# Four graph layers in one kernel: edges on 128 partitions, a bank for layer 1's weights, one record a step at layer 0's end, later outputs in layer 3

## The chip, the cores and the metric

The kernel runs on one core of a Trainium2 chip, in one launch. The time is the device time of that launch in microseconds (us). The kernel before took 3802.98 us as the median of ten runs (3795.99 to 3816.99).

A core has TensorE (PE, matrix products; its weight loads are shown apart as PEld), VectorE (DVE), ScalarE (ACT), GpSimd (POOL) and SyncE (SP). SP and ACT start plain DMAs here. POOL starts the indirect ones: a gather reads one row of a table in device memory for each of up to 128 partitions, by an index that each partition holds, and a scatter writes such rows. [...] Sixteen DMA engines move the data.

## What is computed

A graph of N = 3125 nodes with 256 features and E = 53125 edges, sorted by `dst`, goes through four layers. Each layer reads `h` and its output is added to `x`:

```python
edge_index = jnp.stack([src, dst])
h = jnp.maximum(_layernorm(x, axis=-1), 0.0)
x = x + L0(h, edge_index, edge_attr_64, ...)
h = jnp.maximum(_layernorm(x, axis=-1), 0.0)
x = x + L1(h, edge_index, edge_type_64, ...)
h = jnp.maximum(_layernorm(x, axis=-1), 0.0)
x = x + L2(h, edge_attr_64, ..., edge_index)
h = jnp.maximum(_layernorm(x, axis=-1), 0.0)
x = x + L3(h, edge_index, ...)
```

Cut to what matters here:

```python
# L0: a message for each edge, summed at its dst, then a network for each node
m = relu(concat([h[src], h[dst], edge_attr]) @ eW1 + eb1) @ eW2 + eb2
agg = segment_sum(m, dst)
out = layer_norm(h + mlp(concat([h, agg])), gamma, beta)
# L1: attention with 4 heads and 64 relations, softmax over the edges of a dst
mod_k = K[src] + 0.2 * rel_w[edge_type][:, None, :]
w = softmax over each dst of (Q[dst] * mod_k).sum(-1) / 8
out = layer_norm(segment_sum(w * V[src], dst) @ Wo + bo + h) * gamma + beta
# L2: attention with 8 heads; sums go to the SOURCE side, softmax over all edges
dst, src = edge_index[0], edge_index[1]
key = k[src] + edge_attr @ We + be
out = segment_sum(v[src] * softmax((q[dst] * key).sum(-1) / sqrt(32), axis=0), dst) + bias
# L3: graph attention with one head, then an LSTM step from a zero state
agg = segment_sum(softmax over each dst of leaky_relu(a_src[src] + a_dst[dst]) * xp[src], dst)
i, f, g, o = split(tanh(agg + bias) @ W_ih.T)
out = sigmoid(o) * tanh(sigmoid(i) * tanh(g))
```

## The kernel before

**Two orders of the edges.** Layers 0, 1 and 3 sum at `dst`. The nodes are sorted by degree into 25 blocks of 128, and a node's edges become its slots: for slot s of block b one gather brings one row for each of the block's 128 nodes. Layer 2 sums at the source, so it needs the edges grouped by blocks of 128 sources. For that every edge gets a record of 66 numbers (64 attributes, the address of its dst's row, its source's number in the block), and all records are written into a table `ss` in device memory, source block by source block (`TILES` tiles of 128 records each).

**`prelude`.** The edges lie on `EP` = 125 partitions in `EC` = 425 columns (125 × 425 = 53125). `dst_i`, `e_src`, `e_typ` and `nxt_i` (dst of the next edge, to check the sorting) are loaded so. `counted` (L325 to L334) counts degrees: DVE compares the columns with 128 low and 25 high values (`ol`, `oh`), and PE multiplies the two one-hot sets, a product for each column, in two halves. From the degrees come the rank of every node, the table `a_d` of layer 0's source-side products, the slots (`st`) and `row2`, the place of every edge's record in `ss`. `sfill` fills the whole of `ss` with empty records before, in 40 DMAs from SP. At the end `flag` tells whether the input fits the planned sizes; a branch on it chooses `by_slots` (it does here) or `by_blocks`.

**`by_slots`, the records.** `loaded(c)` loads the attributes of `CH` = 5 columns into a rec buffer by a DMA from SP (L588), `filled` writes the other two fields on DVE (L592, L593), and `scatter_src(n)` (its call of `scatter` is recorded at L158) writes n columns: one indirect scatter for each column, 125 records of 264 bytes, 425 in all. There are two rec buffers; a chunk is loaded at column 1 and filled at column 3 of the one before it. `Kit.queued` keeps POOL's indirect DMAs in the order in which the program writes them, so the places named below are places on POOL's queue.

**Layer 0** runs 226 steps, each for two slots: two gathers `gt` (L154), from the 19th step on one `scatter_src(1)`, four products `ph` on PE (L924), the addition of `gt` to `ph` and the sum into `acc` on DVE (L938, L943), and a `clock.tick()`, by which the node work of earlier blocks goes on in small pieces (`front`, `turned`, `back`). `hp` and `xh` are the node rows that this work loads by SP. When the steps are through, `while clock.busy()` finishes the last block's node work, with `scatter_src(2)` at each tick.

**Layer 1** goes through the slots in 115 shares of up to four gathers `kv` (`scored`), and spreads what is left of the scatters evenly over the shares, less eight that come after the last. `weighed` forms the softmax weights `wt` and the weighted sum: DVE multiplies the weights into kv (L1030), PE adds the slots into `acc` (L1034). `acc` and `wt` are two parts of one PSUM bank, `acc1`. `transposed` turns 128 x 256 node rows through a PSUM tile of its own, `pt`; the products after it use `pm`, two banks.

**Layer 2** reads `ss` by source blocks (`srec`), 594 KB a block. **Layer 3** gathers a row `xg` for each of 439 slots; `block` is a generator that a tick after each gather moves on, each `yield n` letting n ticks pass. It ends with the gated result `gg` (L1457, L1458), `yield 3`, and the scatter to the output, which stands on POOL among the next block's gathers.

Of the kernel before, what the change touches and what calls it, by code (L numbers as in the profile page):

```python
# [9 lines left out]
F32 = mybir.dt.float32  # L10
# [40 lines left out]
assert sum(TILES) == NT  # L51
XH = 516
# [9 lines left out]
class Kit:  # L62
# [67 lines left out]
    def transposed(self, pool, psum, x, name, bufs=2):  # L130

        p = psum.tile([P, 4, P], F32, name="pt", bufs=bufs)
        for k in range(2):
            self.nc.tensor.transpose(p[:, k, :], x[:, k * P:(k + 1) * P], self.ident)  # L134
        t = pool.tile([P, 2, P], F32, name=name)
        self.nc.scalar.copy(t, p[:, 0:2, :])
        return t
# [86 lines left out]
class Lists:  # L224


    def __init__(self, pool):
# [9 lines left out]
        self.row2 = pool.tile([EP, EC], I32, name="row2")  # L237
        self.dst_e = pool.tile([EP, EC], F32, name="dst_e")
        self.srcl_e = pool.tile([EP, EC], F32, name="srcl_e")
# [3 lines left out]
def prelude(ctx, tc, a, a_d, nodes_d, ss, st_d, flag, t):  # L243
# [9 lines left out]
    dst_i = c.tile([EP, EC], I32, name="dst_i")  # L253
    nc.sync.dma_start(dst_i, a["dst"].rearrange("(p c) -> p c", c=EC))
# [5 lines left out]
    e_src = c.tile([EP, EC], I32, name="e_src")  # L260
    nc.scalar.dma_start(e_src, a["src"].rearrange("(p c) -> p c", c=EC))
    e_typ = c.tile([EP, EC], I32, name="e_typ")
    nc.scalar.dma_start(e_typ, a["edge_type_64"].rearrange("(p c) -> p c", c=EC))
    nxt_i = c.tile([EP, EC], I32, name="nxt_i")
    nc.gpsimd.memset(nxt_i, N)
    for p0, p1, w in ((0, EP - 1, EC), (EP - 1, EP, EC - 1)):
        nc.scalar.dma_start(nxt_i[p0:p1, 0:w],
                            bass.AP(tensor=a["dst"].tensor, offset=a["dst"].offset + p0 * EC + 1,
                                    ap=[[EC, p1 - p0], [1, w]]))
# [6 lines left out]
    sfill = c.tile([P, 11, SREC], F32, name="sfill")  # L276
# [12 lines left out]
    nc.gpsimd.memset(cap[:, NB - 1:NB], float(P * TILES[NB - 1]))  # L289
    none = c.tile([1, 512], F32, name="none")  # L290
# [13 lines left out]
    for i in range(40):  # L304
        nc.sync.dma_start(ss[i * 11 * P:(i + 1) * 11 * P, :].rearrange("(p r) c -> p (r c)", p=P),
                          sfill.rearrange("p r c -> p (r c)"))

    both_e = c.tile([EP, EC, 2], I32, name="both_e")
    nc.gpsimd.tensor_copy(both_e[:, :, 0], e_src)
    nc.gpsimd.tensor_copy(both_e[:, :, 1], e_typ)  # L310
    nc.scalar.dma_start(st_d.rearrange("(p c) -> p c", c=2 * EC), both_e.rearrange("p c i -> p (c i)"))


    lo_i = wk.tile([EP, EC], I32, name="lo_i", tag="edge", bufs=4)
    nc.vector.tensor_scalar(lo_i, dst_i, 127, None, op0=ALU.bitwise_and)
    lo = c.tile([EP, EC], BF, name="lo")
    nc.vector.tensor_copy(lo, lo_i)
    hi_i = wk.tile([EP, EC], I32, name="hi_i", tag="edge", bufs=4)
    nc.vector.tensor_scalar(hi_i, dst_i, 7, None, op0=ALU.logical_shift_right)
    hi = c.tile([EP, EC], BF, name="hi")  # L320
    nc.vector.tensor_copy(hi, hi_i)
    pdeg = ps.tile([P, NB], F32, name="pdeg")
    CW = 214

    def counted(hp, c0, c1):  # L325
        w = c1 - c0
        ol = hp.tile([EP, P, CW], BF, name="ol")
        oh = hp.tile([EP, NB, CW], BF, name="oh")
# [4 lines left out]
        for i in range(w):  # L333
            nc.tensor.matmul(pdeg, ol[:, :, i], oh[:, :, i], start=(c0 + i == 0), stop=(c0 + i == EC - 1))  # L334
# [33 lines left out]
    with tc.tile_pool(name="ph", bufs=1) as hp:  # L368
# [3 lines left out]
        counted(hp, CW, EC)  # L372
# [73 lines left out]
    sl_i = wk.tile([EP, EC], I32, name="sl_i", tag="edge", bufs=4)  # L446
    nc.vector.tensor_scalar(sl_i, e_src, 127, None, op0=ALU.bitwise_and)
    nc.vector.tensor_copy(t.srcl_e, sl_i)
    hs_i = wk.tile([EP, EC], I32, name="hs_i", tag="edge", bufs=4)
    nc.vector.tensor_scalar(hs_i, e_src, 7, None, op0=ALU.logical_shift_right)  # L450
    hs = c.tile([EP, EC], BF, name="hs")
    nc.vector.tensor_copy(hs, hs_i)
    eq = op.tile([EP, NB, EC], BF, name="eq")
# [3 lines left out]
    zero = ps.tile([EP, EC], F32, name="zero")  # L457
    nc.vector.memset(zero, 0.0)
    cum = op.tile([EP, NB, EC], F32, name="cum")
# [8 lines left out]
    tots = c.tile([EP, NB], F32, name="tots")  # L468
    nc.vector.tensor_copy(tots, cum[:, :, EC - 1])
    pc3 = ps.tile([P, 4, NB], F32, name="pc3")  # L470
    pc2, pv = pc3[:, 0:2, :], pc3[0:1, 2, :]
    nc.tensor.matmul(pc2[:EP, 0, :], k.tri[:EP, :EP], tots, start=True, stop=True)
    nc.tensor.matmul(pc2[:, 1, :], k.ones[:EP, :], tots, start=True, stop=True)
    viol = wk.tile([EP, EC], F32, name="viol", tag="edge", bufs=4)
    nc.vector.tensor_tensor(viol, dst_i, nxt_i, ALU.is_gt)
    v1 = c.tile([EP, 1], F32, name="v1")
# [5 lines left out]
    nc.vector.tensor_tensor(over, pc2[:, 1, :], cap, ALU.is_gt)  # L482
    v3 = c.tile([P, 1], F32, name="v3")
    nc.vector.tensor_reduce(v3, over, AX.X, ALU.add)
    nc.tensor.matmul(pv[:, 0:1], v1, k.ones[:EP, 0:1], start=True, stop=False)
# [5 lines left out]
    bases = c.tile([EP, NB], F32, name="bases")  # L491
    nc.vector.tensor_scalar(bases, pc2[:EP, 0, :], -1.0, None, op0=ALU.add)
# [4 lines left out]
    for b in range(NB - 1, -1, -1):  # L497
        k.gather(t.st[:, b, 0:SLOTS[b], :].rearrange("p s i -> p (s i)"), flat(st_d, 2 * E), t.off_i[:, b:b + 1], axis=1)
# [46 lines left out]
    pos_i = wk.tile([EP, EC], I32, name="pos_i", tag="edge", bufs=4)  # L545
    nc.vector.tensor_copy(pos_i, cum[:, 0])
    pa_i = wk.tile([EP, EC], I32, name="pa_i", tag="edge", bufs=4)
    nc.vector.tensor_scalar(pa_i, pos_i, 127, None, op0=ALU.bitwise_and)
    pj_i = wk.tile([EP, EC], I32, name="pj_i", tag="edge", bufs=4)
    nc.vector.tensor_scalar(pj_i, pos_i, 7, None, op0=ALU.logical_shift_right)  # L550
    step = wk.tile([EP, EC], F32, name="step", tag="edge", bufs=4)
# [3 lines left out]
    nc.vector.scalar_tensor_tensor(t.row2, hs, float(P * TM), step, op0=ALU.mult, op1=ALU.add)  # L555
    nc.vector.tensor_scalar(t.dst_e, dst_i, float(KVQ), None, op0=ALU.mult)
# [3 lines left out]
def by_slots(ctx, tc, a, out, a_d, nodes_d, ss, t):  # L560
# [19 lines left out]
    attr = a["edge_attr_64"].rearrange("(p c) k -> p c k", c=EC)  # L580
# [16 lines left out]
    def scatter_src(n):  # L597

        for _ in range(n):
            c = done[0]  # L600
            if c == EC:
                return
# [1785 lines left out]
```

## Time and profile before

| what | us |
|---|---|
| median of ten runs | 3802.98 |
| profiled execution | 3803.74 |
| its span | 3801.9 |
| prelude | 0 to 241 |
| layer 0, start and steps | 241 to 1252 |
| layer 0, end | 1252 to 1416 |
| layer 1 | 1416 to 2335 |
| layer 2 | 2335 to 3029 |
| layer 3, node rows | 3030 to 3086 |
| layer 3, edges | 3086 to 3801.9 |

The granted clock of TensorE was 0.779 of full speed on the mean. Over the whole span PE was busy 2401.0 us, DVE 2389.3, ACT 1093.0 and POOL 2481.9, so no engine looks like the bound by its share of 63 to 65%; the stages have different ones. Issuing an indirect DMA costs POOL some 0.30 us more that the profile counts as idle ("issue") and not as busy. A wait line such as "DVE kv L1030 <- PE acc L1034" says that DVE, before an instruction that writes kv at line 1030, stood idle until PE's instruction on acc at line 1034 was done; the numbers after it are the total, how often, and the longest. A DMA issue of `rec` is one plain DMA; its packets are the pieces that the engines move.

### The profile page before, as it was taken

The numbers are of one execution on the slowest core, as the hardware profiler recorded it, in microseconds if no ns is written. First come the engines' busy times: TensorE is split into PE (matmuls) and PEld (weight loads), VectorE is DVE, ScalarE is ACT, GpSimd is POOL, SyncE is SP. The second block draws the span as 40 slices with busy tenths as digits, with TensorE's granted clock in tenths as the row PEclk, the third lists the DMA queues.
The fourth block names the chain that finished last, engine by engine and source line by source line (L and its number), as shares of the span: only waits on it lengthen the run. The fifth ranks groups of instructions, "written<-read, shape, count | busy, mean of one in ns | idle before, by whom it ended". The sixth has DMA issues, their size and how long they took to land. (4 is left out here: it accounts for less than half of the span.)

```text
span 3801.9 us, 32547 instructions
## 1 busy us (share of the span) xinstructions
PE 2401.0 (63%) x9174; PEld 1477.6 (39%) x9174; DVE 2389.3 (63%) x4836; ACT 1093.0 (29%) x2292; POOL 2481.9 (65%) x2497
## 2 busy tenths in 40 slices
PE   5827878788777544677676665898989731112123
PEld 3313434344333223555454443666666520001011
DVE  5646567576666325777777674898988924434444
ACT  1112122222221002222222222676766520112122
POOL 3447677777777775666667553676667446566664
PEclk9858889899998755667877777999999965555556
DMA  6345465665655336666666554666666443333332
GB/s 224 128 128 171 134 182 163 172 181 169 179 168 171 83 93 180 179 189 191 198 184 194 163 160 168 192 202 207 201 207 196 128 128 100 89 99 100 95 103 73
DMA packets 295839, 595.89 MB, mean 157 GB/s; under 512 B 113501, under 2 KB 154508, under 8 KB 295650
## 3 DMA queue, kind: packets, MB, share of 16 engines
q0 software_dynamic: 163616, 472.86, 41.8%
q1 hardware_dynamic: 131512, 119.79, 10.4%
q8 instruction: 76, 1.25, 0.1%
q10 hardware_dynamic: 522, 1.06, 0.1%
q14 instruction: 113, 0.93, 0.1%
HBM read 510.85 MB, written 82.21 MB: 156 GB/s over the span
## 5 line engine op out<-in xcount | busy, mean ns | idle before, releaser
L158 POOL DMA_INDIRECT s_src_records<-rec,row x425 | 512.4, 1206 | 131.6 <-issue 122.5
L154 POOL DMA_INDIRECT kv<-s_l_rows,dst x440 | 456.0, 1036 | 214.5 <-issue 70.4
L924 PE MATMUL ph<-wm,st 128*128 128x512 f32 x904 | 471.0, 648 | 128.5 <-DVE acc L943 61.6
L154 POOL DMA_INDIRECT gt<-s_l_src,srcb x452 | 433.9, 960 | 176.2 <-issue 109.4
L154 POOL DMA_INDIRECT kv<-s_l_kv,st x439 | 419.2, 955 | 177.6 <-issue 107.9
L154 POOL DMA_INDIRECT xg<-s_l_rows,src x439 | 415.7, 947 | 133.7 <-issue 133.7
L1034 PE MATMUL acc<-kv,ident 128*128 128x256 f32 x878 | 305.4, 506 | 118.7 <-DVE kv L1030 118.5
L134 PE MATMUL pt<-ident,hb 128*128 128x128 f32 x50 | 17.0, 442 | 547.0 <-ACT hb L1438 547.0
L938 DVE TENSOR_TENSOR ph<-gt,ph 128x1024 f32<-128x1024 f32 x226 | 276.8, 1225 | 111.8 <-PE ph L924 99.7
L924 PEld LDWEIGHTS ph<-wm,st 128*128 128x128 f32 x904 | 177.0, 206 | 331.2 <-issue 290.0
L1034 PEld LDWEIGHTS acc<-kv,ident 128*128 128x128 f32 x878 | 211.0, 252 | 185.1 <-DVE kv L1030 143.1
L990 PE MATMUL pk<-rel,toh 64*128 64x64 f32 x878 | 163.2, 342 | 157.5 <-DVE mk L992 102.2
L1289 PE MATMUL pg<-kv,oh 128*128 128x256 f32 x880 | 252.9, 413 | 3.7 <-DVE kv L1286 3.4
L943 DVE SCALAR_TENSOR_TENSOR acc<-ph,acc 128x1024 f32<-128x1024 f32 x201 | 245.0, 1219 | 3.0
L985 ACT ACTIVATE toh<-tb,negp 64x512 f32<-64x512 f32 (+3 forms) x119 | 81.8, 687 | 560.4 <-PE pk L990 496.2
L134 PEld LDWEIGHTS pt<-ident,hb 128*128 128x128 f32 x50 | 7.1, 201 | 577.4 <-ACT hb L1438 577.4
L592 DVE COPY rec<-dst_e 125x5 f32<-125x5 f32 x85 | 16.4, 193 | 336.0 <-DMA s_src_records<-rec,row 307.3
L1474 DVE TENSOR_SCALAR sc<-xg,own 128x4 f32<-128x4 f32 (+3 forms) x119 | 29.3, 246 | 314.9 <-DMA xg<-s_l_rows,src 307.5
L990 PEld LDWEIGHTS pk<-rel,toh 64*128 64x128 f32 x878 | 146.2, 248 | 203.3 <-issue 139.8
L1431 DVE SCALAR_TENSOR_TENSOR acc<-xg,sc,acc 128x256 f32<-128x256 f32 x439 | 211.7, 487 | 6.9
L1244 PE MATMUL pk<-we,eat 64*128 64x256 f32 x880 | 161.9, 441 | 43.2 <-DVE mk L1250 41.7
L1289 PEld LDWEIGHTS pg<-kv,oh 128*128 128x128 f32 x880 | 156.6, 198 | 53.7 <-DVE kv L1286 31.3
(373 smaller groups left out, 5405.1 us busy)
## 6 DMA issues: line engine op xcount, KB each, us to landing
s_src_records<-sfill SPq DMA_DIRECT2D x40, 363.0 KB
srec<-s_src_records SPq DMA_DIRECT2D x24, 594.0 KB
rec<-in_edge_attr_dram SPq DMA_DIRECT2D x85, 156.2 KB
tb<-s_slot_types SPq DMA_DIRECT2D x101, 128.0 KB
gt<-s_l_src,srcb POOLq DMA_INDIRECT x452, 3.6
kv<-s_l_rows,dst POOLq DMA_INDIRECT x440, 3.8
kv<-s_l_kv,st POOLq DMA_INDIRECT x439, 3.8
xg<-s_l_rows,src POOLq DMA_INDIRECT x439, 2.8
```

Source lines behind the costliest of these rows:

```text
L154: self.queued(lambda: self.nc.gpsimd.indirect_dma_start(out=to, out_offset=None, in_=table, in_offset=bass.IndirectOffsetOnAxis(ap=index, ...
L158: st = self.queued(lambda: self.nc.gpsimd.indirect_dma_start(out=table, out_offset=bass.IndirectOffsetOnAxis(ap=index, axis=0), in_=rows, ...
L924: nc.tensor.matmul(ph[:, h, :], stat[h][:, s % 4, :], ms[b][h], start=True, stop=True)
L938: nc.vector.tensor_add(ph, gt, ph)
L943: nc.vector.scalar_tensor_tensor(accs[b], ph, 0.0, accs[b], op0=ALU.max, op1=ALU.add)
L985: nc.scalar.activation(to, tb[:, 0:n * P], AF.Abs, bias=negp[:64])
L990: nc.tensor.matmul(pk[:, q, :], toh[:, q, :], rel, start=True, stop=True)
L1034: nc.tensor.matmul(acc, ident, v[:, q, :], start=(s0 + q == 0), stop=(s0 + q == C - 1))
L1244: nc.tensor.matmul(pk[:, i, :], eat[i * 64:(i + 1) * 64, q, :], we[i * 64:(i + 1) * 64, :], start=True, stop=True)
L1289: nc.tensor.matmul(pg, oh[:, j % T6 + i, :], v[:, i, :], start=(j + i == 0), stop=(j + i == n - 1))
L1431: nc.vector.scalar_tensor_tensor(acc, xgs[q // U3][:, q % U3, 0:D], s[:, q:q + 1], acc, op0=ALU.mult, op1=ALU.add)
L1474: nc.vector.tensor_scalar(sc[:, q0:q1], xg[:, 0:q1 - q0, 256], own[:, 257:258], None, op0=ALU.add)
```

## The change

The edges now lie on all 128 partitions in `ECW` = 416 columns. 127 partitions are full, and the last holds `EL` = 53125 − 127 × 416 = 293 edges; the rest of its columns is filled with numbers that match no node. So 416 scatters of 128 records are issued instead of 425 of 125. The records of the empty places go to 128 rows that `ss` has more. Each load of an edge array becomes a DMA for 127 partitions and one for the last, and POOL fills the array before. `counted` does 208 columns in each half.

`sfill` writes only the last three tiles of each source block, and the flag's check also asks that every block fills the tiles before them (`low`). `CH` is 4, there are three fixed rec buffers, and a load stands two chunks ahead: at column 3 of a chunk for the chunk after the next; the fill stays one chunk ahead, at column 1. In layer 1 `wt` has a bank `wt1`, and `transposed` takes its tile from the two of `pm`. The ticks at layer 0's end issue one scatter each: 53 there instead of 105; layer 1 then issues 156 instead of 113. In layer 3 the last `yield` is 9 instead of 3.

In the diff's main parts:

```diff
+ECW = 416
+EL = E - (P - 1) * ECW
+FULL = (15,) * (NB - 1) + (5,)
...
-    def transposed(self, pool, psum, x, name, bufs=2):
+    def transposed(self, pool, psum, x, name, tag="pt"):
...
-    dst_i = c.tile([EP, EC], I32, name="dst_i")
-    nc.sync.dma_start(dst_i, a["dst"].rearrange("(p c) -> p c", c=EC))
+    def edges(engine, to, of):
+        engine.dma_start(to[0:P - 1, :], of[0:(P - 1) * ECW].rearrange("(p c) -> p c", c=ECW))
+        engine.dma_start(to[P - 1:P, 0:EL], of[(P - 1) * ECW:E].rearrange("(p c) -> p c", p=1))
+    dst_i = c.tile([P, ECW], I32, name="dst_i")
+    nc.gpsimd.memset(dst_i, 32 * P)
+    edges(nc.sync, dst_i, a["dst"])
...
+    past = c.tile([1, ECW - EL], I32, name="past")
+    nc.gpsimd.iota(past, pattern=[[1, ECW - EL]], base=NT * P, channel_multiplier=0)
...
-    for i in range(40):
-        nc.sync.dma_start(ss[i * 11 * P:(i + 1) * 11 * P, :].rearrange("(p r) c -> p (r c)", p=P),
-                          sfill.rearrange("p r c -> p (r c)"))
+    for b0, b1_ in ((0, 12), (12, NB - 1), (NB - 1, NB)):
+        n = TILES[b0]
+        r0 = b0 * P * TM
+        nc.sync.dma_start(ss[r0:r0 + (b1_ - b0) * P * n, :].rearrange("(b p j) c -> p b (j c)", p=P, j=n)
+                          [:, :, FULL[b0] * SREC:n * SREC],
+                          sfill.rearrange("p r c -> p (r c)")[:, None, :].to_broadcast([P, b1_ - b0, 3 * SREC]))
...
+    nc.vector.tensor_tensor(low, low, pc2[:, 1, :], ALU.is_gt)
+    nc.vector.tensor_add(over, over, low)
...
+    nc.sync.dma_start(t.row2[P - 1:P, EL:ECW], past)
...
-    CH = 5
-    recs = ctx.enter_context(tc.tile_pool(name="s_recs", bufs=2))
+    CH = 4
+    recs = ctx.enter_context(tc.tile_pool(name="s_recs", bufs=1))
+    ring_ = [recs.tile([P, CH, SREC], F32, name=f"rec{i}") for i in range(3)]
+    for rec in ring_:
+        nc.gpsimd.memset(rec, 0.0)
...
     def loaded(c):
-        rec = recs.tile([EP, CH, SREC], F32, name="rec")
-        nc.sync.dma_start(rec[:, :, 0:64], attr[:, c:c + CH, :])
-        return rec
+        rec = ring_[c // CH % 3]
+        last = (P - 1) * ECW
+        nc.sync.dma_start(rec[0:P - 1, :, 0:64], attr[0:last, :].rearrange("(p c) k -> p c k", c=ECW)[:, c:c + CH, :])
+        w = min(CH, EL - c)
+        if w > 0:
+            nc.sync.dma_start(rec[P - 1:P, 0:w, 0:64], attr[last + c:last + c + w, :].rearrange("(p c) k -> p c k", p=1))
...
             if c == 0:
-                rec_of[0] = loaded(0)
-                filled(0, rec_of[0])
-            if c % CH == 1 and c0 + CH < EC:
-                rec_of[c0 + CH] = loaded(c0 + CH)
-            if c % CH == 3 and c0 + CH < EC:
-                filled(c0 + CH, rec_of[c0 + CH])
-            k.scatter(ss, row2[:, c:c + 1], rec_of[c0][:, c % CH, :], "src_records")
+                loaded(0)
+                filled(0)
+                loaded(CH)
+            if c % CH == 1 and c0 + CH < ECW:
+                filled(c0 + CH)
+            if c % CH == 3 and c0 + 2 * CH < ECW:
+                loaded(c0 + 2 * CH)
+            k.scatter(ss, row2[:, c:c + 1], ring_[c // CH % 3][:, c % CH, :], "src_records")
...
         while clock.busy():
             clock.tick()
-            scatter_src(2)
+            scatter_src(1)
...
-            bank = ps.tile([P, 512], F32, name="acc1", bufs=1)
-            acc = bank[:, 0:D]
-            wt = bank[:, D:D + 4 * C].rearrange("p (s h) -> p s h", h=4)
+            acc = ps.tile([P, 512], F32, name="acc1", bufs=1)[:, 0:D]
+            wt = ps.tile([P, 512], F32, name="wt1", bufs=1)[:, 0:4 * C].rearrange("p (s h) -> p s h", h=4)
...
-            mst = k.transposed(wk, ps, ms, "mst", 1)
+            mst = k.transposed(wk, ps, ms, "mst", "pm")
...
-                ht = k.transposed(wk, ps, h, "ht", 1)
+                ht = k.transposed(wk, ps, h, "ht", "pm")
...
             nc.vector.tensor_add(gg, gg, own[:, 258:XPR])
-            yield 3
+            yield 9
             n = rows(b)
             k.scatter(out, nid_i[:n, b:b + 1], gg[:n], "out")
```

## The prediction

> **What bounds the kernel now.** I read the times first, then the busy time of each engine by stage, then, stage by stage, who waits for whom, and last the DMA queues. Times are us of the profiled execution: 3803.74 in all, a span of 3801.9 and 1.8 around it. The median of the ten runs is 3802.98, so the profile stands for it and I add changes to the median. By stage (columns: stretch, its length, busy time of PE, its weight loads, DVE, ACT, POOL with instruction counts, granted clock, DMA share, GB/s):
>
> ```profile
> 0.00:241.00 241.00, 127.47 (x689) 70.68 (x689) 142.09 (x597) 40.61 (x110) 100.73 (x156) 0.81 0.43 147
> 280.00:1252.00 972.00, 787.25 (x2302) 394.41 (x2301) 619.98 (x875) 208.11 (x424) 734.09 (x709) 0.90 0.59 169
> 1252.00:1415.60 163.60, 79.82 (x191) 45.99 (x189) 41.72 (x140) 15.12 (x35) 129.70 (x111) 0.64 0.30 73
> 1415.60:2333.00 917.40, 603.57 (x2158) 434.92 (x2158) 649.43 (x1041) 222.16 (x368) 580.95 (x577) 0.72 0.60 176
> 2335.00:3029.00 694.00, 606.03 (x3391) 427.58 (x3391) 599.95 (x1198) 454.01 (x1041) 455.99 (x440) 0.94 0.62 199
> 3086.00:3801.00 715.00, 145.41 (x250) 69.44 (x250) 294.94 (x883) 121.30 (x242) 464.02 (x489) 0.56 0.34 95
> ```
>
> The rows are the prelude, layer 0's steps, its end, layer 1, layer 2 and layer 3's edges. In layer 0 POOL is busy 734.09 of 972, and each of its 709 transfers costs 0.30 more to issue (213), so it is taken for 947 of 972: POOL sets the step. In layer 0's end it is taken for 129.70 + 111 × 0.30 = 163 of 163.6. In layer 1 it is 581 + 577 × 0.30 = 754 of 917, in layer 3 464 + 489 × 0.30 = 611 of 715; the rest there is waiting. The prelude hangs on the edges: DVE and PE count degrees one after the other.
>
> The groups that the change touches on POOL (busy total, mean ns of one, idle before):
>
> ```profile
> L158 POOL DMA_INDIRECT s_src_records<-rec,row x425 | 512.4, 1206 | 131.6 <-issue 122.5 <-DVE rec L593 2.9 <-DMA kv<-s_l_kv,st 2.1
> ...
> L158 POOL DMA_INDIRECT out_dram<-gg,nid_i x25 | 25.5, 1020 | 103.7 <-DVE gg L1458 91.6 <-DVE one L1426 10.9 <-issue 1.2
> L158 POOL DMA_INDIRECT s_l_kv<-kv,nid_i x25 | 25.2, 1009 | 7.6 <-issue 7.0 <-DMA gt<-s_l_src,srcb 0.3 <-DVE y L818 0.3
> L158 POOL DMA_INDIRECT s_l_rows<-row,nid_i x25 | 25.1, 1004 | 124.6 <-DVE row L1094 54.3 <-DVE den L1017 23.9 <-DVE sc L1008 18.7
> ```
>
> The same helper writes 125 rows in 1206 ns and 128 rows in about 1000. One of the 25 out scatters has 53 rows and takes 1567. So the number of rows, not their sum of bytes, sets the price. Waits (total, times, longest), first in the prelude, then in layer 1, then in layer 3:
>
> ```profile
> DVE lo_i L315 <- DMA dst_i<-in_dst_dram: 6.4, 1, 6.4
> ...
> DVE kv L1030 <- PE acc L1034: 57.5, 41, 3.9
> ...
> POOL kv L154 <- PE acc L1034: 45.4, 32, 23.1
> ...
> POOL out_dram L158 <- DVE gg L1458: 91.6, 19, 11.1
> ```
>
> The DMA queues from 600 to 900, in the middle of layer 0 (packets, MB, share of 16 engines; then an issue group):
>
> ```profile
> q0 software_dynamic: 15679, 43.87, 51.1%
> q1 hardware_dynamic: 15066, 8.65, 10.0%
> ...
> rec<-in_edge_attr_dram SPq DMA_DIRECT2D x13, 156.2 KB
> ```
>
> **The odd rows.** Packet by packet the trace shows how a transfer is spread. A load of 128 rows runs on sixteen engines; dst_i's 125 rows never have more than five packets at once (76 ns each); xh's last load, 53 rows, has one at a time, 46 ns apart. A rec load of before is 625 packets of 256 B at 18 ns on five engines: 625 × 0.018 / 5 = 2.3 us, about 3.1 under layer 0's traffic. These three counts go with the largest divisor up to sixteen. The changed loads have 127 rows, prime like 53, so I take one engine: 127 × 4 = 508 packets × 0.018 = 9.1 us for four columns, all on one engine. This is the term that speaks against the change; the lower bound is the row of 125 (five engines, under 2 us).
>
> [...] No run shown here has 127. [...]
>
> **Prelude and start of layer 0.** The first xh load now stands ahead of dst on SP, and dst's 127 rows take 127 × 0.076 = 9.7 us on one engine that it shares with e_src's and e_typ's equal loads from ACT. So dst lands near 25 us rather than 7, and DVE starts some 18 later; waits further on (25.7 for the last counts) move along, so I take +15 (with five engines +3). Nine columns less of 425 in the counting: 2% of some 60 us, −1. The 123 place numbers that SP copies into row2 after the last DVE instruction stand before the branch: one small DMA, +3 (0 to +4). In the first 30 us of layer 0 three rec loads, 27 us of one engine, stand on SP ahead of the second hp load, which the first products need; in before the two first rec loads stand there with 2.3 each. At most 27 − 5 = +22, at least 0; part of it is under weight loads, which keep the engines 0.7 busy there, so +12. Filling only the last three tiles of ss takes 37 DMAs from SP and 12 MB from 18 to 71 us; DVE and PE count meanwhile, and nothing waits for it: 0. The new memsets on POOL lie in its 91.7 us wait: 0; SP waits for one of them under 1 us. Sum +29 (+2 to +40).
>
> **Layer 0's steps.** 207 scatters are issued there in both kernels. Each is 1206 − 1004 = 0.20 cheaper: −42, all of it on the path as long as POOL is the bound. Against it: the engines are 61.1% busy; without the 13 rec loads (146 us of the 4800) 58%, 174 us of 300. The engine that also carries 16.75 rec loads a 300 us has 153 more: 327 of 300. With each gather packet at its shortest (159 ns for 4 KB where many take 400) the 174 are about 140, and 293 of 300 fits. So the loads land at the pace of the step, or up to 9% behind it (930 us × 9% = +84). They are issued five steps ahead (5 × 4.2 = 21 us) for about 18 when the engine is shared evenly. DVE's two fills of a rec buffer come three steps after its load is issued (about 13 us), and now wait for that load instead of for an earlier scatter (174.5 us of DVE waits in these steps before). Queued behind a fill on DVE are the additions to ph and the sums acc; they free the gt buffers that POOL's gathers need, five steps deep. Behind a rec load on SP stand hp and xh of the next block. With these covers I take that three quarters of the gain go: −10 (−42 to +84).
>
> **Layer 0's end.** 53 scatters instead of 105, and six others: 53 × 1.30 + 8 = 77 of POOL instead of 162. But 53 columns need 13 rec loads, 121 us of that engine; two are there beforehand (−18), other traffic (30% of the engines) takes some back: about 130. So −32 (−85 without that limit, 0 if the node work itself needs the 163).
>
> **Layer 1.** The 52 scatters left out arrive here less nine that are gone: 113 × 1.51 = 171 before, 156 × 1.30 = 203 after, +32 on POOL, which is 82% taken. The weights in their own bank take away DVE's 57.5 behind PE's products, of which POOL feels 45.4 through its kv buffers: −30. The transposes now share the two banks of pm; DVE waits 26 + 23 for that ring now, so +5. 39 rec loads are 355 of an engine that is 60% busy of 917 (550): 905 of 917, tight, +5 (0 to +60). Sum +12 (−35 to +95). Layer 2 reads the same records: 0.
>
> **Layer 3.** Every out scatter stands six gathers later. POOL waits 102.5 for gg and one; the last three (8.4, 7.9, 8.5 by the waits one by one) come after the last gather and stay; six gathers at 0.947 + 0.30 = 1.25 cover 7.5 each of the other 77, of which four waits are longer (8.4, 11.1, 9.9, 8.7) and leave 8. That is −69; DVE, which is 41% busy here and waits 307.5 for gathers, may finish a block later where POOL no longer pauses, so I take −60 (−70 to −35).
>
> **Sum.** +29 − 10 − 32 + 12 − 60 = −61: 3742.
>
> **Rivals.** First: the loads are spread or hidden as before. Speaks for it the deeper prefetch; against it the 53 rows. Prelude +2, layer 0 −42, its end −85, layer 1 +2, layer 3 −60: −183, 3620. Second, slower: the one engine becomes layer 0's and layer 1's bound. Place: rec loads on SP's queue; every other transfer of sixteen engines waits for its share on that engine too. Price: +40, +84, 0, +60, −60 = +124, 3927; half of the two large terms gives 3855. It decides once the engine's own work passes the step, 9.1 us + 58% of four steps (16.6 us) = 18.7 against 16.6: by packet times it does, by shortest times it does not. It ends slower than before where layers 0 and 1 lose more than about 65. Third: layer 3's wait only moves (data instead of gg), and the rest cancels: 3800.
>
> **How the numbers follow.** 0.47 for the forecast (own range 3690 to 3785), 0.17 for the first rival, 0.29 for the second, 0.07 for the third. The time is the likeliest's, 3742. The range leaves out some 0.1 at each end: 3635 to 3880. A difference of 0.2% (7.6 us) is about what can be told from none. Faster: the forecast and the first rival, 0.63; same 0.08, the third with edges of its neighbours; slower 0.29.
>
> **What would show it.** Right: the group of the record scatter near 1000 ns; DVE's first wait for dst near 24; a rec load landing in 9 us or more; layer 3's POOL wait for gg below 40; layer 0's end near 130. Wrong: rec loads landing in 3 us; DVE or POOL in layer 0 waiting for rec's DMA in most chunks and steps above 4.2 us; out scatters still waiting 90.

## The result and the profile after

The changed kernel takes 3831.68 us (median of 11 runs, 3825.13 to 3842.01) against 3803.58 of the kernel before (37 runs): a ratio of 1.0077, 95% interval 1.0067 to 1.0087. It is 28 us slower, where 61 us faster was forecast; the range held it.

The two profiled executions, cut at the same events (first gather `gt`, first addition to `ph`, last `gt`, layer 1's first `kv`, layer 2's first and last `kv`, first `xg`, end of the last output scatter), beside the prediction's terms:

| stage, us | before | after | change | predicted |
|---|---|---|---|---|
| prelude | 241.5 | 272.5 | +31 | +17 |
| layer 0, start | 31.6 | 46.4 | +15 | +12 |
| layer 0, steps | 978.2 | 935.9 | −42 | −10 |
| layer 0, end | 164.2 | 158.1 | −6 | −32 |
| layer 1 | 934.9 | 986.9 | +52 | +12 |
| layer 2 | 652.1 | 661.0 | +9 | 0 |
| layer 3, node rows | 83.8 | 84.8 | +1 | 0 |
| layer 3, edges | 708.3 | 675.0 | −33 | −60 |

The same stages as busy time of each engine, in the changed kernel (columns as in the prediction's windows):

```profile
0.00:272.50 272.50, 128.29 (x680) 72.36 (x680) 140.88 (x603) 41.06 (x111) 101.07 (x165) 0.82 0.28 89
319.00:1254.90 935.90, 781.22 (x2319) 393.01 (x2319) 627.88 (x900) 211.11 (x427) 699.87 (x713) 0.92 0.60 176
1254.90:1413.00 158.10, 74.82 (x193) 42.73 (x191) 40.74 (x127) 15.02 (x35) 57.15 (x60) 0.65 0.18 53
1413.00:2399.80 986.80, 568.48 (x2170) 440.27 (x2171) 650.76 (x1079) 225.91 (x379) 603.94 (x620) 0.68 0.58 173
...
3145.70:3820.70 675.00, 141.19 (x250) 68.23 (x250) 285.37 (x883) 124.66 (x244) 468.16 (x488) 0.56 0.36 101
```

The prelude does the same work (DVE 140.88 us against 142.09) in 31 us more, so the rest is waiting. (The fall from 147 to 89 GB/s doesn't show it: `sfill` writes some 12 MB less there.) Layer 0's steps are what the cheaper scatter gives: POOL 699.87 for 713 instructions plus 713 × 0.30 of issue is 914 of 935.9. At layer 0's end POOL is busy for 57 of 158 us, 75 with its issues: it no longer binds, and the stage is hardly shorter. Layer 1 has 43 more instructions on POOL (620 against 577) and 23 us more of busy time, but lasts 52 longer.

The scatter groups after (busy total, mean ns, idle before):

```profile
L162 POOL DMA_INDIRECT s_src_records<-rec,row x416 | 417.5, 1003 | 158.3 <-issue 117.3 <-DVE rec L623 21.2 <-DMA rec<-in_edge_attr_dram 13.6
...
L162 POOL DMA_INDIRECT out_dram<-gg,nid_i x25 | 25.7, 1026 | 66.0 <-DVE gg L1485 52.0 <-DVE one L1453 10.4 <-issue 2.4
L162 POOL DMA_INDIRECT s_l_kv<-kv,nid_i x25 | 24.6, 982 | 56.5 <-DVE kv L884 50.1 <-issue 6.4
```

128 rows take 1003 ns, as forecast. The output scatter's wait falls from 103.7 only to 66.0. The scatter of layer 1's node rows (`s_l_kv`) now waits 50.1 us for DVE; those waits are all at layer 0's end.

That the loads of 127 rows run on one engine, and what this costs, is seen in two places, the prelude and layer 0's start. From 10 to 20 us the DMA view has its 40 rates in GB/s, and then the plain queue's packets, MB and share:

```profile
GB/s 20 47 80 217 268 186 184 350 387 372 385 376 213 98 96 36 27 27 20 27 27 20 27 27 20 27 20 27 27 20 27 27 20 27 27 20 27 27 20 27
...
q1 hardware_dynamic: 807, 0.86, 28.4%
```

The rate stands at 20 to 27 GB/s while dst, src and the types come in, in packets of 1664 bytes that take 69 ns (median), nearly always one at a time: 24 GB/s. The kernel before never falls under 90 in that stretch. DVE's waits in the prelude (total, times, longest):

```profile
DVE ol L350 <- PE pdeg L354: 23.2, 1, 23.2
...
DVE lo_i L335 <- DMA dst_i<-in_dst_dram: 15.3, 1, 15.3
```

dst comes 14 us later (the first compare starts at 22.2 instead of 7.9). The other half of the prelude's loss is a step that the prediction did not have: PE's queue has the products of a bias row, `b`, ahead of the first counts. That row stands on SP behind xh and `w1a`, and SP, held behind dst's loads, has issued the first four xh loads only at 36 us instead of 13. PE's first work, before and then after:

```profile
25.18 3.75 PE L361 MATMUL pa<-b,ones 1*128 1x512 f32 x4 [25.18 <-DMA b<-in_L_gnn_eb_dram]
```

```profile
51.81 3.75 PE L381 MATMUL pa<-b,ones 1*128 1x512 f32 x4 [51.81 <-DMA b<-in_L_gnn_eb_dram]
```

So PE starts the counts at 55.5 instead of 28.9, and the second half of DVE's compares waits 23.2 for PE instead of 9.6. The second place is layer 0's start. SP's issues (start, how long the issue took):

```profile
282.58 0.27 SPq L615 DMA_DIRECT2D rec<-in_edge_attr_dram  x1
285.04 11.96 SPq L618 DMA_DIRECT2D rec<-in_edge_attr_dram  x1
297.09 0.37 SPq L615 DMA_DIRECT2D rec<-in_edge_attr_dram  x1
297.51 6.70 SPq L618 DMA_DIRECT2D rec<-in_edge_attr_dram  x1
304.30 0.36 SPq L615 DMA_DIRECT2D rec<-in_edge_attr_dram  x1
304.76 7.14 SPq L727 DMA_DIRECT2D hp<-s_nodes  x1
```

L615 is the load of 127 rows, L618 that of the one row. Here whatever SP issues next after a load of 127 rows is held for 7 to 12 us; the `hp` load that the first products need is out of SP at 312 instead of 271.

Most experiments ran where the kernel before itself took 4196 to 4264 us, and only e13 and e14 where it took 3812.97, near the first comparison; so each ratio below is to the kernel before beside it, and stages are compared within one of the two groups, unless both are named.

### The profile page after: what moved, and what is told of

The parts are those of the page before. It is cut to its first block, busy times and chain, and to the rows that moved or that the text cites. A ratio compares the mean times of both kernels' runs of the same rounds, so it can differ in the third digit from the quotient of the medians.

```text
span 3831.4 us, 32661 instructions
## 1 busy us (share of the span) xinstructions
PE 2348.8 (61%) x9165; PEld 1479.0 (39%) x9165; DVE 2377.8 (62%) x4876; ACT 1097.3 (29%) x2296; POOL 2403.5 (63%) x2497
## 5 line engine op out<-in xcount | busy, mean ns | idle before, releaser
L162 POOL DMA_INDIRECT s_src_records<-rec,row x416 | 417.5, 1003 | 158.3 <-issue 117.3
L1019 PE MATMUL pk<-rel,toh 64*128 64x64 f32 x878 | 182.2, 369 | 282.4 <-DVE mk L1021 165.5
L967 DVE TENSOR_TENSOR ph<-gt,ph 128x1024 f32<-128x1024 f32 x226 | 276.9, 1226 | 112.8 <-PE ph L953 102.9
L1019 PEld LDWEIGHTS pk<-rel,toh 64*128 64x128 f32 x878 | 163.1, 273 | 316.3 <-issue 191.3
L1061 PE MATMUL acc<-kv,ident 128*128 128x256 f32 x878 | 243.4, 445 | 50.5 <-DVE kv L1057 50.5
L622 DVE COPY rec<-dst_e 128x4 f32<-128x4 f32 x104 | 19.6, 191 | 345.5 <-DMA s_src_records<-rec,row 320.2
L1061 PEld LDWEIGHTS acc<-kv,ident 128*128 128x128 f32 x878 | 197.8, 229 | 89.0 <-DVE kv L1057 53.8
L1277 DVE TENSOR_TENSOR mk<-kv,pk 128x512 f32<-128x512 f32 x220 | 149.5, 680 | 52.6 <-DMA kv<-s_l_rows,dst 41.9
```

The source lines that it names most:

```text
L162: st = self.queued(lambda: self.nc.gpsimd.indirect_dma_start(out=table, out_offset=bass.IndirectOffsetOnAxis(ap=index, axis=0), in_=rows, ...
L967: nc.vector.tensor_add(ph, gt, ph)
L1019: nc.tensor.matmul(pk[:, q, :], toh[:, q, :], rel, start=True, stop=True)
L1061: nc.tensor.matmul(acc, ident, v[:, q, :], start=(s0 + q == 0), stop=(s0 + q == C - 1))
L1277: nc.vector.tensor_add(mk, o.kv[j // 2][:, :, 0:D], pk)
```

## The experiments

**Spread the record loads (e1).** The load takes all 128 partitions while the last one still has edges for the chunk, and 112 + 15 + 1 after that.

```diff
-        nc.sync.dma_start(rec[0:P - 1, :, 0:64], attr[0:last, :].rearrange("(p c) k -> p c k", c=ECW)[:, c:c + CH, :])
...
+        for p0, p1, n in ((0, P, CH),) if w == CH else ((0, 112, CH), (112, P - 1, CH), (P - 1, P, w)):
+            if n > 0:
+                nc.sync.dma_start(rec[p0:p1, 0:n, 0:64],
+                                  bass.AP(tensor=attr.tensor, offset=attr.offset + (p0 * ECW + c) * 64,
+                                          ap=[[ECW * 64, p1 - p0], [64, n], [1, 64]]))
```

> The changed kernel, but a chunk's attributes come by one load of 128 partitions while the last partition still has four edges in it (columns 0 to 291), and by 112 + 15 + 1 partitions after that. One-engine theory: what layer 0's start, its end and layer 1 lost against the prediction is the load of 127 partitions, which runs on one engine and holds SP 8 us behind it. Then the start of layer 0 is 10 to 20 us shorter, its end 20 to 60, layer 1 20 to 50: about 3757 in all (3720 to 3790). Rival, scatters moved: layer 1 is longer because it issues 43 more scatters and the node chain sets layer 0's end whatever the loads do; then only the start gains and the time is 3812 to 3835.

**Spread the edge arrays (e2)**, the next dst likewise.

```diff
-        engine.dma_start(to[0:P - 1, :], of[0:(P - 1) * ECW].rearrange("(p c) -> p c", c=ECW))
+        engine.dma_start(to[0:112, :], of[0:112 * ECW].rearrange("(p c) -> p c", c=ECW))
+        engine.dma_start(to[112:P - 1, :], of[112 * ECW:(P - 1) * ECW].rearrange("(p c) -> p c", c=ECW))
```

> The changed kernel, but dst, src, types and the next dst are loaded on 112 + 15 + 1 partitions instead of 127 + 1. One-engine theory: dst lands near 7 to 9 us, the layer 1 weights of the first product come off SP earlier, and the whole prelude ends 20 to 25 us earlier: 3807 to 3815. Rival, the order on the queues (memsets before the loads, xh ahead of dst): under 8 us are gained, 3824 to 3836.

**The changed kernel as yardstick (e5), both spread (e6, and again e15).**

> The changed kernel as it is, as the yardstick beside the other three of this call. If this chip runs like the one of the first comparison, the ratio to the kernel before is 1.005 to 1.010; if it runs like the chip of the last four, 1.02 to 1.035.

> The changed kernel with the record loads on 128 partitions (112 + 15 + 1 at the end) and the edge arrays on 112 + 15 + 1. One-engine theory: against the changed kernel the prelude is 25 to 30 us shorter, the start of layer 0 15 to 20, its end 20 to 30, layer 1 0 to 30: ratio to the changed kernel 0.970 to 0.984, on a chip like the first 3725 to 3770. Rival, moved scatters and the node chain: only the first two, 0.988 to 0.991.

> The kernel of e6 once more: the changed kernel with its loads spread. On a chip like the first: prelude 28 us and start of layer 0 15 us shorter than in the changed kernel, the end of layer 0 20 to 25, layer 1 8 to 20: 3745 to 3765, ratio to the kernel before 0.982 to 0.988; then the single record a tick costs another 40 to 55 us beside e14's two. Rival, the single record costs nothing: within 10 us of e14's 3707.

Ratios: e1 1.0171 (1.0105 to 1.0237), e2 1.0255 (1.021 to 1.0299), e5 1.0287 (1.0203 to 1.0371), e6 1.0116 (1.0033 to 1.0198), e15 1.0057 (1.0024 to 1.0089). e5 and e6 stood side by side: the loads cost the changed kernel 1.7% by the ratios, and by the medians it takes 0.981 of its time with both spread, inside the 0.970 to 0.984 that the one-engine theory expected. The absolute times forecast for a chip like the first could not be compared. By stage, in us:

| | prelude | start | steps | end | layer 1 |
|---|---|---|---|---|---|
| e5, 127 + 1 everywhere | 279.3 | 47.6 | 1086.0 | 157.0 | 1184.1 |
| e2, edge arrays spread | 244.2 | 46.1 | 1101.6 | 158.9 | 1182.8 |
| e1, records spread | 272.0 | 28.8 | 1079.6 | 133.1 | 1175.4 |
| e6, both | 245.3 | 32.4 | 1091.0 | 134.7 | 1176.9 |
| e15, both | 252.8 | 27.4 | 1101.2 | 132.5 | 1199.3 |

Each load gives back where it stands: the arrays about 30 us of prelude, the records 15 to 20 of the start and 24 of layer 0's end. In the steps and in layer 1 nothing moves beyond the scatter of these runs: the 20 to 50 us that the theory expected in layer 1 did not come here, as its rival said. DVE's longest group of waits at layer 0's end, in the changed kernel and then in e6:

```profile
DVE rec L622 <- DMA s_src_records<-rec,row: 78.4, 14, 8.4
```

```profile
DVE rec L624 <- DMA s_src_records<-rec,row: 37.7, 12, 4.8
```

The line is right as it stands: DVE's fill waits for the last scatter out of the same buffer, three chunks back, and not for its own load. The load comes in one step earlier. In the changed kernel (SP, POOL, DVE):

```profile
1307.10 0.30 SPq L615 DMA_DIRECT2D rec<-in_edge_attr_dram  x1
1307.44 7.27 SPq L618 DMA_DIRECT2D rec<-in_edge_attr_dram  x1
1314.88 0.29 SPq L615 DMA_DIRECT2D rec<-in_edge_attr_dram  x1
1318.06 0.97 POOL L162 DMA_INDIRECT s_src_records<-rec,row  x1 [2.43 <-DMA rec<-in_edge_attr_dram]
1325.98 0.17 DVE L622 COPY rec<-dst_e 128x4 f32<-128x4 f32 x1 [3.65 <-DMA s_src_records<-rec,row]
```

In the stage a load goes out every 7 to 8 us. Packet by packet, and from the stage's second chunk on, the first of a chunk's four scatters starts 1.7 to 2.2 us after its load's last packet, and 10 us or more after its fill; so it waits for the load. (The profile names the load in some of these waits and a fill of another chunk in the others.) The fill shown is the next one of the same buffer: it waits for these scatters, and the node work behind it on DVE waits too. The last of the 53 scatters starts 99 us into the stage, and 59 us of node work follow without any. With the loads spread (e6) these are 75 and 60: the loads cost the first part alone.

**The bank of layer 1 undone (e3 in the changed kernel, e8 in the one with both loads spread).**

```diff
-            acc = ps.tile([P, 512], F32, name="acc1", bufs=1)[:, 0:D]
-            wt = ps.tile([P, 512], F32, name="wt1", bufs=1)[:, 0:4 * C].rearrange("p (s h) -> p s h", h=4)
+            bank = ps.tile([P, 512], F32, name="acc1", bufs=1)
+            acc = bank[:, 0:D]
+            wt = bank[:, D:D + 4 * C].rearrange("p (s h) -> p s h", h=4)
...
-            mst = k.transposed(wk, ps, ms, "mst", "pm")
+            mst = k.transposed(wk, ps, ms, "mst", "pt", 1)
...
```

> The changed kernel with layer 1's weights back in the bank of the sums, and the transposes back in a tile of their own. Theory of the prediction: the bank was worth 25 to 35 us in layer 1, so this takes 3855 to 3868. Rival, the bank is off the path while POOL and late loads set layer 1: 3824 to 3842. Rival, sharing pm with the transposes costs more than the bank gives: below 3822.

> The kernel with both kinds of loads spread, and layer 1's weights back in the bank of the sums, the transposes in a tile of their own. Theory of the prediction: 25 to 35 us longer in layer 1 than with the bank. Rival, the bank is off the path: within 8 us of it. Rival, pm shared with the transposes costs more: shorter by 8 us and more.

e3: 1.0297 (1.0252 to 1.0342); e8: 1.0118 (1.0037 to 1.0199). By the whole time neither is parted from its neighbour (e5 1.0287, e6 1.0116). By the stage they are, narrowly: layer 1 takes 1207.5 and 1204.6 with the shared bank, 1175 to 1199 (five runs, above) with its own, so the bank, with the transposes in pm, is worth some 5 to 32 us, 22 between the means (1206.1 and 1183.7).

**The place of the scatters.** e11 is the kernel before with one scatter a tick; e9 has both loads spread and takes the same edit back to two.

```diff
         while clock.busy():
             clock.tick()
-            scatter_src(2)
+            scatter_src(1)
```

> The kernel before with one scatter instead of two at each tick of layer 0's end, and nothing else. Theory, moved scatters: the end falls from 165 to 132 to 142 us, where the node work itself binds, and layer 1 grows by 50 to 75: ratio to the kernel before 1.004 to 1.012. Rival, layer 1 has room for them (its POOL waits over 200 us): ratio 0.992 to 0.999.

> The kernel with both kinds of loads spread, with two scatters instead of one at each tick of layer 0's end. Theory, moved scatters: layer 1's extra time is the 43 more scatters that the end left to it; the end is bound by POOL again and grows from 135 to 145 to 165 us, layer 1 falls by 40 to 60; 15 to 40 us faster than with one scatter a tick. Rival, the shared pm banks and the fills on DVE make layer 1 longer: layer 1 falls by under 20 and the whole is not faster.

e11: 1.006 (1.0016 to 1.0104). e9: 1.0004 (0.9966 to 1.0042), against 1.0116 and 1.0057 with one scatter a tick. Layer 0's end and layer 1 in e11, then in e9:

```profile
1368.50:1495.40 126.90, 70.03 (x196) 38.65 (x194) 41.23 (x123) 15.12 (x35) 68.80 (x59) 0.74 0.26 65
1495.40:2685.50 1190.10, 646.25 (x2170) 459.38 (x2171) 652.85 (x1068) 225.12 (x377) 645.76 (x629) 0.66 0.50 144
```

```profile
1362.90:1536.20 173.30, 77.56 (x197) 42.94 (x195) 44.31 (x155) 15.13 (x35) 108.08 (x112) 0.66 0.24 68
1536.20:2664.70 1128.50, 578.65 (x2170) 444.04 (x2171) 650.03 (x1053) 225.84 (x379) 552.29 (x569) 0.66 0.50 148
```

In the kernel before, one scatter a tick takes 38 us from the end (164.5 in e4's trace) and adds 53 to layer 1 (1136.8 there; 39 or 63 against e17 or e7, where it took 1151.2 or 1126.8): 52 scatters are 78 us of POOL (52 × 1.51), of which the end gave up half and layer 1 paid some two thirds. In e9 layer 1 falls by 48 from e6 and the end grows by 39, to more than the 145 to 165 expected; the whole ratio fell by more than these stages give, and the rest isn't placed (layer 2 varied by 40 us between these runs).

**Later fills (e10 with one scatter a tick, e12 and e16 with two).**

```diff
-            if c % CH == 1 and c0 + CH < ECW:
+            if c % CH == 3 and c0 + CH < ECW:
                 filled(c0 + CH)
```

> The kernel with both kinds of loads spread, with the two fills of a record buffer two scatters later (four scatters behind the load's issue instead of two). Theory, the fills hold DVE: its waits at the fills (91 us in all) fall below 40, layer 0's end is 5 to 15 us shorter and layer 1 5 to 20. Rival, those waits are covered by other work: within 8 us.

> All that the runs so far speak for: both kinds of loads spread, the weights in their own bank, two scatters a tick at layer 0's end, layer 3's later scatter, and the fills of a record buffer four scatters behind its load. Against the kernel before on the same chip: if the fills held the node work at layer 0's end, the end falls from 173 us to 145 to 160, and the ratio is 0.985 to 0.999 on a chip like those of the experiments, 0.970 to 0.982 on one like that of the first comparison. Rival, the fills are covered: ratio 0.997 to 1.004 on a chip like those of the experiments.

> The kernel of e12 once more: e14's with the fills of a record buffer four scatters behind its load. On a chip like the first: if fills hold the node work at layer 0's end, 5 to 20 us faster than e14's 3707; if not, within 5 us of it.

e10: 1.0092 (1.0056 to 1.0128); e12: 1.001 (0.9976 to 1.0045); e16: 1.0009 (0.9981 to 1.0037). All as without the later fill; the end takes 131.5, 174.1 and 173.2. DVE's waits at the fills for earlier scatters fell only from 91.0 (e6) to 70.0 (e10), not below 40: the fill waits for a scatter, and moving it two scatters on takes away a part. That part gave no time, so the theory fell; a kernel without these waits was not tried.

**The later output scatter alone (e4, e7, e17: the kernel before with `yield 9`).**

> The kernel before with layer 3's last yield 9 instead of 3 and nothing else. If the later scatter alone made layer 3's gain in the changed kernel's trace (35 us of 712), this takes 3765 to 3772. The prediction's full cover of the waits would give 3738 to 3750. If part of the gain came from elsewhere: above 3780.

> The kernel before with layer 3's last yield 9 instead of 3, once more. If the later scatter made the 35 us of layer 3 in the changed kernel's trace: ratio to the kernel before 0.990 to 0.992. If it gains nothing by itself: 0.998 to 1.004.

> The kernel before with the last yield 9 and nothing else, on a chip like the first: 30 to 38 us faster than the kernel before if the later scatter alone makes layer 3's gain; 60 and more as predicted; under 10 if the gain needs the other parts.

1.003 (1.0009 to 1.005), 0.9997 (0.9954 to 1.0041), 0.9974 (0.9938 to 1.0009): no gain where these ran. There layer 3's edges took 746 to 749 us with the later scatter, and DVE got behind POOL (in e4 POOL's waits for gg come to 102.9 us, the longest 25.2); the last section has its trace. e13 answers it where the kernel before took 3812.97.

**The columns apart (e13, the kernel before with the bank and the later scatter; e14, the kernel of e9, beside it).**

> The kernel before with layer 1's weights in a bank of their own (the transposes in pm) and layer 3's last yield 9, on 125 partitions as before. Theory: layer 1 falls by 20 to 30 us, layer 3 by nothing (as with the later scatter alone on such a chip) or 35 (as in the first comparison): ratio to the kernel before 0.992 to 0.996 or 0.982 to 0.988. Rival, the bank's gain in layer 1 is lost again behind it: 0.997 to 1.003.

> The kernel of e9 once more, beside e13: it differs from it by the 416 columns, their ring of three buffers, the shorter fill of the record table and the spread loads. Theory, POOL binds layer 0's steps: 25 to 50 us faster than e13. Rival, on such a chip DVE binds the steps: within 12 us of e13.

e13: 3759.18 us, 0.986 (0.9845 to 0.9876). e14: 3707.42 us, 0.9722 (0.9709 to 0.9736), faster than both kernels of this study. Layer 0's steps, its end and layer 1 in e13, with layer 3's edges last:

```profile
279.40:1256.00 976.60, 791.45 (x2320) 397.05 (x2319) 626.20 (x880) 210.22 (x427) 736.18 (x712) 0.90 0.60 169
1256.00:1420.30 164.30, 80.50 (x193) 46.16 (x191) 41.71 (x139) 15.11 (x35) 130.38 (x111) 0.64 0.31 73
1420.30:2340.80 920.50, 563.59 (x2170) 437.20 (x2171) 650.15 (x1051) 225.29 (x379) 581.16 (x577) 0.69 0.62 182
3075.00:3747.00 672.00, 140.37 (x250) 68.21 (x250) 285.38 (x883) 124.72 (x244) 463.59 (x488) 0.56 0.37 101
```

and the first three of them in e14:

```profile
275.30:1215.40 940.10, 786.08 (x2320) 396.30 (x2319) 627.09 (x900) 211.24 (x427) 701.80 (x712) 0.91 0.61 175
1215.40:1372.50 157.10, 79.99 (x193) 44.91 (x191) 43.06 (x153) 14.88 (x35) 108.46 (x111) 0.64 0.26 75
1372.50:2285.10 912.60, 560.00 (x2170) 434.03 (x2171) 650.05 (x1053) 225.69 (x379) 553.28 (x568) 0.70 0.62 183
```

The bank takes 14 us from layer 1 (934.9 to 920.5) and the later scatter 36 from layer 3, with nothing else changed (one trace of each). The columns, with their loads spread, then take 36.5 us from the steps, 7 from the end and 8 from layer 1, and their whole, 51.8 us, is just above the 25 to 50 expected.

e14 differs from the changed kernel by the spread loads and two scatters a tick. Beside the changed kernel's first profile its prelude is 26 us shorter and its start 17.6, as in the experiments on the loads. Layer 1 is 74 us shorter, which is more than the place of the scatters was worth above (48 in e9). So some 20 to 30 us of layer 1 stay open: where the loads were spread alone, nothing could be seen in layer 1, but that was in the other group of runs.

## Why the prediction was wrong, step by step

The forecast was −61 and the measurement +28. The terms miss by +17 (prelude and start together), −32 (steps), +26 (layer 0's end), +40 (layer 1), +10 (layer 2 and the node rows) and +27 (layer 3): +88 in sum.

**One engine for 127 rows: right, and priced in the wrong stages.** It was argued from the rows of 125 and 53 and is shown by e1 and e2. But the prediction let it eat three quarters of the steps' gain, and it ate none: 935.9 us with the loads on one engine, 940.1 with them spread (e14). The term was mis-sized and its wait misread. A load was priced at 9.1 us of the engine; the three at layer 0's start took 7.1 to 7.8 from first packet to last. In the steps a load's last packet came 9.8 to 14.6 us after its issue, and a chunk's first scatter stood some 20 us behind that (median). The wait was to be DVE's fills, which "now wait for that load": in the steps the median fill starts 12 us before its own load has landed, and DVE's waits there still name scatters (161.1 us, 174.5 before). The two sums, 327 and 293 of 300 us, left it open whether the engine binds; the second, with each packet at its shortest, came nearer. (By the same shortest times the rival's comparison is 9.1 + 47% of 16.6 = 16.8 against 16.6, not below it, as the prediction says.) The changed kernel's trace agrees with one engine for 127 rows: in the prelude the packets of these loads come nearly always one at a time, at 20 to 27 GB/s.

**Prelude and start, +29 predicted, +46 measured.** The delay of dst was sized well (18 and 14). Left out was what stands behind it on SP: the bias row that PE needs ahead of its first counts (26.6 us later). And the queue holds: SP itself was blocked 7 to 12 us by the load before, which the prediction, counting only the engine, did not have.

**Layer 0's end, −32 predicted, −6 measured.** The step "77 of POOL, 130 for the loads" took the longer of the two for the whole stage and had no term for the node work, though "0 if the node work itself needs the 163" was kept as a bound. The loads' part was even shorter than 130: the last scatter starts at 99 us. But 59 us of node work stand behind it, with no scatter left to cover. The same 58 to 60 us stand there in e1, e5 and e6; with the loads out of the way the stage takes 133 to 135 (e1, e6, e15), and 127 with one scatter a tick in the kernel before (e11). The node work behind the last scatter is the term that was put at nothing.

**Layer 1, +12 predicted, +52 measured: the step that failed most.** "+32 on POOL, −30 for the bank" set one against the other at about equal size. The +32 for 43 scatters counted POOL's own time. e11 shows that 52 scatters moved into layer 1 cost it 53 us by themselves (by proportion 44 for the 43 of the change), in a stage where POOL had idle time to spare, so that time was no room. The bank's 30 was too large: 14 in e13, 22 on average in e3 and e8. DVE's waits behind PE's products (57.5) do go, but POOL still waits for PE's sums with the bank alone (47.6 in e13, 45.4 before). Then 44 less 14 is 30 of the 52. The other 22, an estimate across the two groups of runs, stay open: "+5" for the loads may be too small, as e14 leaves room for it, and DVE waits 62.3 us for the landing of the gathers of layer 1 in the changed kernel against 31.2 in e14 and 48.1 before. No run parts the loads from the scatters there.

**Layer 3, −60 predicted, −33 measured.** The later scatter does alone what the trace shows (−36 in e13). The step "six gathers cover 7.5 each of the other 77" took every wait by itself. In the trace the waits before the last gather fall from 79 to 40.6, and the first one grows from 8.4 to 10.3, though its scatter stands six gathers later: the result itself comes later, 118 us after layer 3's first gather instead of 107. DVE's queue has scores of those further gathers ahead of it:

```profile
3245.40 0.23 DVE L1501 TENSOR_SCALAR sc<-xg,own 128x4 f32<-128x4 f32 x1 [2.17 <-DMA xg<-s_l_rows,src]
3250.46 0.23 DVE L1501 TENSOR_SCALAR sc<-xg,own 128x4 f32<-128x4 f32 x1 [4.44 <-DMA xg<-s_l_rows,src]
3255.75 0.23 DVE L1501 TENSOR_SCALAR sc<-xg,own 128x3 f32<-128x3 f32 x1 [4.67 <-DMA xg<-s_l_rows,src]
```

So the gathers that were to cover the wait also put the result off. The prediction allowed 9 us for a DVE that finishes later; some 33 were needed. That reading is the trace's and was not tried by itself.

**The rivals.** The second, slower one was nearest in sign, but its mechanism, the engine as the bound of layers 0 and 1, did not happen. The loss came from queues behind the loads and from work moved between stages. Of the signs that were to show the forecast right, three came (a record scatter of 1003 ns, dst at 22.2, loads landing 9.8 us and more after their issue in the steps) and two did not: POOL's wait for gg fell to 52.0, not below 40, and layer 0's end to 158, not near 130.

**Filling less of the record table** was costed at nothing, and nothing in the stages contradicts it: e14's prelude, with its loads spread, takes 246.5 and e13's, which fills all, 247.5.

## What to carry to other kernels

An odd row out was dear here: 127 + 1 rows put the loads on one engine and cost some 70 us (1.7% where the kernel before took 4198), 128 or 112 + 15 + 1 rows gave them back, and the queue that the loads stood on paid (8.2 us for SP's next issue, median), not only their reader. Work taken out of a stage that POOL bound paid only down to the next chain in that stage (38 us of the 78 in e11), and was paid for where it landed (some two thirds of it), even in a stage with idle POOL time; so price both ends before moving it, and look for work in the stage that nothing overlaps. For a chain of waits between two engines, don't add up what each wait could shrink: look at what the producer itself waits for.

## What the runs showed of the hardware

In the changed kernel a load on one engine held the queue that issued it: SP's next issue took 8.2 us on the median (74 one-row loads, up to 12.0), where its other issues mostly take 0.3 to 0.6; in layer 0's steps that came to 444 us of SP without costing the steps anything.

The time of the gathers' landing rose from 3.6 to 5.0 us (median) in the changed kernel with no loss in the steps:

```profile
gt<-s_l_src,srcb POOLq DMA_INDIRECT x452, 5.0
```

Where the kernel before took 4196 to 4264 us, DVE was late with its own instructions. In this stretch of e4's layer 3 it starts an instruction of 0.49 us every 1.4 to 2.1 us, with waits that the profile puts down to nothing in the program ("remote", or the instruction before):

```profile
3553.30 0.49 DVE L1431 SCALAR_TENSOR_TENSOR acc<-xg,sc,acc 128x256 f32<-128x256 f32 x1 [0.90 <-issue]
3555.41 0.49 DVE L1431 SCALAR_TENSOR_TENSOR acc<-xg,sc,acc 128x256 f32<-128x256 f32 x1 [1.62 <-remote]
3557.50 0.49 DVE L1431 SCALAR_TENSOR_TENSOR acc<-xg,sc,acc 128x256 f32<-128x256 f32 x1 [1.61 <-remote]
3558.90 0.49 DVE L1431 SCALAR_TENSOR_TENSOR acc<-xg,sc,acc 128x256 f32<-128x256 f32 x1 [0.91 <-DVE acc L1431]
```

All runs of that group have 456 to 582 us of DVE waits put down to "remote"; the kernels before and after, e13 and e14 have none. There POOL's gains vanish: the columns gave the steps nothing (1086.0 in e5, 1078 to 1085 in e4, e7 and e17) and the later scatter gave layer 3 nothing. What delays DVE there was not found; the expectations speak of the chip, but the record has chip 7 on runs of both groups (e1 to e4 and e15 to e17, and e13 and e14).
